# Four banks for a tile's sums, one run of new values, and a new order within a slot

## The chip, the cores and the metric

The kernel runs on one core of a Trainium2 chip. The metric is the device time of one execution in microseconds (us), the median of the runs shown. Times of single instructions are often given in nanoseconds (ns).

## The reference, cut to what matters

Four residual layers in a row over x of 64 batches x 32 rows x 512 features. The first and the last mix channels with a matrix chosen per batch, the second is a linear layer with a low-rank correction chosen per batch, and the third, where nearly all of the time goes, is attention with a paged cache:

```python
q = rope(rmsnorm(x @ Wq.T))        # 32 heads of 128; k and v have 8 heads
k, v = rope(rmsnorm(x @ Wk.T)), x @ Wv.T
k_all = concat(k_cache[block_table], k)   # 512 cached keys (16 pages of 32) + 32 new ones
v_all = concat(v_cache[block_table], v)
scores = where(valid, q @ k_all.T / sqrt(128), -1e30)
o = softmax(scores) @ v_all        # four query heads share one key head
x = x + o @ Wo.T
```

All data is fp32.

## The kernel before, in words

**Tiles, units, slots.** A tile is 128 rows of x, that is four batches. The key heads are done in two groups of four, so there are 2 x 16 = 32 steps of one group on one tile. A step has four units, one for each batch (`j` from 0 to 3), and a unit has four slots, one for each key head `k` of the group. A slot therefore handles one batch and one key head with its four query heads: 128 query rows (4 heads x 32 rows) against 544 keys. There are 32 x 4 x 4 = 512 slots, and the whole attention is one long list of them. In this text a slot is numbered by its place in that list; 16 slots make a tile, four make a unit.

**A slot's own pipeline.** `scores` (L832) makes 128 x 544 scores with two matmuls into a PSUM tile of two banks, `s_ps`, of which there is one; VectorE then adds the mask, and finds each row's extreme, in one pass (L846, called "the top" below: a pass of 128 x 544 with a short read of its accumulator), and ScalarE takes the exponential (L857). `divide` (L859) takes the reciprocal on VectorE (L862) and scales the cached part (L863) and the new part (L864) on ScalarE. Two slots later `flip` (L877) transposes the probabilities in four 128 x 128 pieces into the one bank `pT_ps` (tag "t" of the pool `ps_t`), and VectorE copies them to SBUF (L882). Three slots later `values` (L884) multiplies with the cached values in four accumulating matmuls (L893).

**What is done once in a unit.** `flip_new` (L866) transposes the new keys' probabilities of all four heads, in one 128 x 128 piece, into columns 0 to 127 of the *current* slot's score tile, which the scores leave unused; ScalarE copies them out (L875). It stands in the slot whose number is 1 modulo 4. `values_new` (L901) adds the new keys' values: four matmuls of 32 rows each (L905), one for each head, from four different row ranges into four different sums. `finish` (L913) copies the four sums to SBUF on ScalarE (L919, L922). After the fourth unit `store` (L927) writes the tile's 1 MB to DRAM with one DMA, on SP's queue except in the last three steps.

**PSUM.** Two banks hold the scores, one the flipped probabilities (tag "t"), one the projections (`proj_ps`), three the sums of the heads 0 to 2 (tag "o"), and the last one (tag "o3") is shared by the sum of head 3, the transposes of the query and key heads (`head_ps`, L750) and those of the second group's cache pages (`pageT_ps`, L266).

**What is interleaved.** Between these, the same slots carry the projections of the next pair of tiles. `Block.project` (L644) issues one matmul of 128 x 512 at a time (L651), one or two in nearly every slot. `Norm` (L697) turns the projected rows into normalized, rotated heads: squares on ScalarE (L707), a power on GpSimd (L712, L714), then the VectorE passes `scale`, `straight`, `swapped` and `sum` (L719 to L748, "pieces" below), the four transposes of `turn` (L756) and a copy on ScalarE, `keep` (L768).

**What sets the order.** The order is written out by hand, and every engine takes its instructions in the order in which the program issues them. `at(slot, where, ...)` puts a call into a plan and `slot(i)` (L1193) runs the plan for one slot, with these lines in the middle:

```python
            new.scores(k)
            turned.flip((i - LAG) % KG)
            run(i, "pe")                      # projections
            run(i, "take"); run(i, "late"); run(i, "power"); norm_piece(i)
            turned.flip_new()                 # every fourth slot
            run(i, "turn")                    # transposes of heads and pages
            old.values((i - VLAG) % KG)       # VLAG = 3, LAG = 2
            old.values_new()                  # every fourth slot, then at(i, "act", old.finish)
            new.divide(k)
            run(i, "dve"); norm_piece(i); norm_piece(i); run(i, "dve")
            run(i, "keep"); run(i, "act"); run(i, "store")
```

Two more places matter: GpSimd's queue gathers a unit's cached values, four gathers of 128 rows (`fetch_values`, L800, shown as L105), with eight buffers `v_sb` for two units; and SP's queue loads the cached keys page by page (L794) and a unit's new values (`fetch_new`, L813).

After the attention the output projection runs alone (L1301 to L1414).

## Time and profile before

| | |
|---|---|
| runs shown | 2476.70, 2469.84, 2477.28 us |
| their median | 2476.7 us |
| the profiled execution's own time | 2473.52 us |
| its span in the profile | 2471.8 us, so 1.7 us lie around it |
| TensorE clock granted | 0.999 |
| busy: TensorE matmul, weight load | 2438.3 us (99%), 1855.4 us (75%) |
| busy: VectorE, ScalarE, GpSimd | 1609.2 us (65%), 1398.3 us (57%), 1174.2 us (48%) |

The profile is of one execution. It has the busy time of each engine, a chain of waits that is followed back from the last instruction, groups of equal instructions with their mean durations, and a timeline. In it PE is TensorE's matmul, PEld TensorE's load of weights, DVE VectorE, ACT ScalarE, POOL GpSimd, SP SyncE; `s_ps L841` is what line 841 writes into the tile `s_ps`. An fp32 matmul shows as two matmuls, each with its own load of weights; a transpose shows as one. The durations of matmuls overlap, since they are pipelined: what one costs is read from the distance of the starts.

### The profile page before, as it was taken

The numbers are of one execution on the slowest core, as the hardware profiler recorded it, in microseconds if no ns is written. First come the engines' busy times: TensorE is split into PE (matmuls) and PEld (weight loads), VectorE is DVE, ScalarE is ACT, GpSimd is POOL, SyncE is SP. The second block draws the span as 40 slices with busy tenths as digits, with TensorE's granted clock in tenths as the row PEclk, the third lists the DMA queues.
The fourth block names the chain that finished last, engine by engine and source line by source line (L and its number), as shares of the span: only waits on it lengthen the run. The fifth ranks groups of instructions, "written<-read, shape, count | busy, mean of one in ns | idle before, by whom it ended". The sixth has DMA issues, their size and how long they took to land.

```text
span 2471.8 us, 47357 instructions
## 1 busy us (share of the span) xinstructions
PE 2438.3 (99%) x13760; PEld 1855.4 (75%) x13760; DVE 1609.2 (65%) x3602; ACT 1398.3 (57%) x4135; POOL 1174.2 (48%) x1096
## 2 busy tenths in 40 slices
PE   7999999999999999999999999999999999999999
PEld 4556777777777777777777777777777788888887
DVE  5767767676767677777777777777776756433222
ACT  2236767676767767677777777777676754000000
POOL 4436555455555565655556555555555753000000
PEclk9999999999999999999999999999999999999999
DMA  7876666666667677756666666565667784333221
GB/s 237 293 231 199 188 198 191 193 195 189 202 188 209 188 218 220 250 180 194 178 189 176 185 179 186 171 192 173 187 178 220 252 258 155 117 112 129 86 86 60
DMA packets 448545, 459.19 MB, mean 186 GB/s; under 512 B 51424, under 2 KB 379488, under 8 KB 440480
## 3 DMA queue, kind: packets, MB, share of 16 engines
q1 hardware_dynamic: 398384, 291.24, 38.1%
q0 software_dynamic: 49904, 164.93, 22.2%
q8 instruction: 112, 1.84, 0.3%
q14 instruction: 145, 1.19, 0.2%
HBM read 384.66 MB, written 79.69 MB: 188 GB/s over the span
## 4 chain that ended last, share of the span: by engine, by line
PE 95%; DMA 2%; issue 2%; SPq 1%; DVE 0%; POOL 0%; ACT 0%; DVEq 0%; POOLq 0%; ACTq 0%
PE proj_ps L651 23%; PE o_ps L893 18%; PE out_ps L1323 15%; PE s_ps L838 11%; PE s_ps L841 9%; PE pT_ps L880 9%; PE l_ps L490 3%; PE head_ps L756 3%; PE o_ps L905 2%; DMA kT<-kT 1%; PE h_ps L474 1%; SPq L794 1%; PE s_ps L873 1%; PE mix_ps L1341 1%; PE mix_ps L435 1%
## 5 line engine op out<-in xcount | busy, mean ns | idle before, releaser
L105 POOL DMA_INDIRECT v_sb<-v,v_rows x512 | 538.1, 1051 | 352.7 <-PE o_ps L893 242.8
L846 DVE CUSTOM_DVE_ANT_0 sm<-s_ps,pen 128x544 f32<-128x544 f32 x512 | 370.9, 724 | 457.9 <-PE s_ps L841 337.2
L893 PEld LDWEIGHTS o_ps<-pT,v_sb 128*128 128x128 f32 x4096 | 519.2, 192 | 133.6 <-issue 126.3
L857 ACT ACTIVATE sm<-sm,top 128x544 f32<-128x544 f32 x512 | 381.8, 746 | 339.6 <-DVE top L846 266.2
L893 PE MATMUL o_ps<-pT,v_sb 128*128 128x128 f32 x4096 | 541.4, 275 | 2.5 <-issue 1.3
L863 ACT ACTIVATE sm<-sm,share 128x512 f32<-128x512 f32 x512 | 369.8, 722 | 175.9 <-DVE share L862 144.2
L882 DVE COPY pT<-pT_ps 128x512 f32<-128x512 f32 x512 | 351.5, 687 | 8.0 <-PE pT_ps L880 4.1
L838 PE MATMUL s_ps<-kT,qT 128*128 128x288 f32 x1024 | 347.0, 420 | 2.8 <-DMA kT<-kT 2.1
L880 PE MATMUL pT_ps<-ident,sm 128*128 128x128 f32 x2048 | 307.7, 273 | 0.6 <-DVE pT L882 0.6
L841 PE MATMUL s_ps<-kT,qT 128*128 128x256 f32 x1024 | 305.3, 380 | 2.4 <-DMA kT<-kT 2.4
L880 PEld LDWEIGHTS pT_ps<-ident,sm 128*128 128x128 f32 x2048 | 256.1, 141 | 52.5 <-DVE pT L882 1.0
L809 POOL TENSOR_SCALAR pen<-key_f,seq_f 128x544 f32<-128x544 f32 x128 | 285.0, 2227 | 11.6 <-issue 0.3
L712 POOL TENSOR_SCALAR ss<-ss 128x4 f32<-128x4 f32 x160 | 56.4, 353 | 438.1 <-ACT sq L707 437.5
L841 PEld LDWEIGHTS s_ps<-kT,qT 128*128 128x128 f32 x1024 | 194.4, 190 | 57.2 <-issue 2.0
L663 DVE TENSOR_TENSOR raw<-proj_ps,raw 128x512 f32<-128x512 f32 x332 | 223.4, 685 | 18.7 <-PE proj_ps L651 13.9
L707 ACT ACTIVATE sq<-raw 128x128 f32<-128x128 f32 x640 | 197.2, 308 | 18.5 <-DVE raw L663 2.3
L714 POOL TENSOR_TENSOR rstd<-ss,minus_half 128x4 f32<-128x4 f32 x160 | 185.1, 1157 | 13.4
L1373 ACT COPY p<-out_ps 128x256 f32<-128x256 f32 x7 | 2.6, 373 | 333.1 <-PE out_ps L1323 333.1
L651 PE MATMUL proj_ps<-sum,x 128*128 128x512 f32 x380 | 186.9, 594 | 0.0
L105 POOL DMA_INDIRECT mix_rows<-in_w,cond_rows x32 | 33.0, 1031 | 309.3 <-DVE mix_diag L171 299.5
L838 PEld LDWEIGHTS s_ps<-kT,qT 128*128 128x128 f32 x1024 | 154.7, 191 | 20.0 <-issue 3.5
L1323 PE MATMUL out_ps<-w,o_in 128*128 128x256 f32 x768 | 167.1, 379 | 0.0
(175 smaller groups left out, 3492.7 us busy)
## 6 DMA issues: line engine op xcount, KB each, us to landing
kT<-kT SPq DMA_DIRECT2D x2048, 64.0 KB
o<-oT SPq DMA_DIRECT2D x29, 1024.0 KB
o_in<-o SPq DMA_DIRECT2D x28, 1024.0 KB
page_rows<-in_kv_cache SPq DMA_DIRECT2D x32, 256.0 KB
v<-in_kv_cache SPq DMA_DIRECT2D x32, 256.0 KB
kT<-page_rows SPq DMA_DIRECT2D x32, 256.0 KB
vn<-raw SPq DMA_DIRECT2D x32, 256.0 KB
v_sb<-v,v_rows POOLq DMA_INDIRECT x512
```

What stands on the lines that cost most here:

```text
L105: nc.gpsimd.indirect_dma_start(out=dst, out_offset=None, in_=table, in_offset=bass.IndirectOffsetOnAxis(ap=index, axis=0),)
L651: nc.tensor.matmul(self.ps, lhsT=self.pair.x[x][:, c if x == "b" else half.start + c, :], rhs=blocks(self.b)[w][:, c, :], start=(c == 0), ...
L809: nc.gpsimd.tensor_scalar(self.pen, key_f, seq_f[:, self.b : self.b + 1], BIG, ALU.is_ge, ALU.mult)
L838: nc.tensor.matmul(ps[:, first:HID], lhsT=q, rhs=self.kT[:, :n1, k, :], start=True, stop=True)
L841: nc.tensor.matmul(ps[:, HID : first + LA], lhsT=q, rhs=self.kT[:, n1:, k, :], start=True, stop=True)
L846: nc.vector.tensor_tensor_reduce(out=sm, in0=ps[:, first : first + LA], in1=self.pen, scale=1.0, scalar=3e38, op0=ALU.add, op1=ALU.min, ac ...
L857: nc.scalar.activation(sm, sm, AF.Exp, bias=top, scale=-1.0, accum_out=total)
L863: nc.scalar.activation(sm[:, :L], sm[:, :L], AF.Copy, scale=share)
L880: nc.tensor.transpose(ps[:, c, :], self.sm[k][:, c * P : (c + 1) * P], ident)
L882: nc.vector.tensor_copy(pT, ps)
L893: nc.tensor.matmul(self.o_ps[k], lhsT=self.v[c][:, k * D : (k + 1) * D], rhs=self.pT[k][:, c, :], start=(c == 0), stop=False,)
L1323: nc.tensor.matmul(ps[:, :HALF], lhsT=o[:, i, :], rhs=w[i // REP][:, i % REP, :], start=(i == 0), stop=(i == KG * REP - 1),)
```

## The change

- **Sums.** Each head of a tile has a bank of its own (tags o0 to o3) for all four units: `[128, 4, 128]`, one column range for each unit. Only the first matmul of a tile in a bank sets `start`.
- **New values in one go.** `values_new` is called for the four units one after the other, after the last `values` of the tile: 16 matmuls in a row, once in 16 slots, instead of four once in four slots. `v_new` and `pT_new` get four buffers each, and `fetch_new` is moved to the slots 4, 7, 10 and 13 of its tile.
- **finish and store.** They are called for each head of the tile: one copy of 128 x 512 each, two in the slot of the new values and two in the next one, to tiles `oT` of 256 KB with three buffers; four DMAs of 256 KB, those of the heads 0 and 1 on SP's queue and those of 2 and 3 on GpSimd's.
- **Order in a slot.** `values` (and `values_new`) come directly after the scores, then `flip_new`, `flip`, `divide`, and only then the projections and, last on TensorE, the transposes of heads and pages.
- **Bank.** Those transposes now use the bank of the flipped probabilities (tag "t"). The rule that kept them out of the slots of a unit's last head is gone.

```diff
--- before.py
+++ after.py
@@ -265,7 +265,7 @@
 
             def turn(self):
                 if self.g:
-                    self.ps = room["o"].tile([P, HID], F32, name="pageT_ps", tag="o3")
+                    self.ps = ps_t.tile([P, HID], F32, name="pageT_ps", tag="t")
                 else:
                     self.ps = ps_s.tile([P, 2 * HID], F32, name="s_ps")
                 for k in range(KG):
@@ -748,10 +748,7 @@
                 nc.vector.tensor_tensor(self.a, self.a, self.b, ALU.add)
 
             def turn(self):
-                if "o" in room:
-                    self.tp = room["o"].tile([P, REP, P], F32, name="head_ps", tag="o3")
-                else:
-                    self.tp = ps_t.tile([P, REP, P], F32, name="head_ps", tag="t")
+                self.tp = ps_t.tile([P, REP, P], F32, name="head_ps", tag="t")
                 for h in range(REP):
                     nc.tensor.transpose(self.tp[:, h, :], self.a[:, h, :], ident)
 
@@ -812,7 +809,7 @@
 
             def fetch_new(self):
 
-                self.v_new = room["v"].tile([P, D], F32, name="v_new", bufs=2)
+                self.v_new = room["v"].tile([P, D], F32, name="v_new", bufs=NB)
                 nc.sync.dma_start(
                     out=self.v_new,
                     in_=vn_dram[self.g][self.t][self.j * S : (self.j + 1) * S, :].rearrange(
@@ -827,7 +824,7 @@
                     step_of[self.s].kT_new[:, self.j].rearrange("p k s -> p (k s)"),
                 )
                 self.new = room["attn"].tile([P, KG, S], F32, name="p_new")
-                self.sm, self.total, self.pT, self.o_ps = {}, {}, {}, {}
+                self.sm, self.total, self.pT = {}, {}, {}
 
             def scores(self, k):
 
@@ -871,7 +868,7 @@
                 else:
                     ps = ps_s.tile([P, 2 * HID], F32, name="s_ps")[:, :P]
                 nc.tensor.transpose(ps, self.new.rearrange("p k s -> p (k s)"), ident)
-                self.pT_new = room["attn"].tile([P, P], F32, name="pT_new", bufs=1)
+                self.pT_new = room["attn"].tile([P, P], F32, name="pT_new", bufs=NB)
                 nc.scalar.copy(self.pT_new, ps)
 
             def flip(self, k):
@@ -884,18 +881,16 @@
             def values(self, k):
 
 
-                if k == 0:
-                    self.o_three = room["o"].tile([P, KG - 1, HID], F32, name="o_ps", tag="o")
-                    self.o_ps = {i: self.o_three[:, i, :P] for i in range(KG - 1)}
-                elif k == KG - 1:
-                    self.o_ps[k] = room["o"].tile([P, HID], F32, name="o_ps3", tag="o3")[:, :P]
+                if self.j == 0:
+                    o_of[self.s, k] = room["o"].tile([P, NB, P], F32, name="o_ps", tag=f"o{k}")
                 for c in range(NC):
                     nc.tensor.matmul(
-                        self.o_ps[k],
+                        o_of[self.s, k][:, self.j, :],
                         lhsT=self.v[c][:, k * D : (k + 1) * D],
                         rhs=self.pT[k][:, c, :],
-                        start=(c == 0),
+                        start=(self.j == 0 and c == 0),
                         stop=False,
+                        skip_group_check=True,
                     )
 
             def values_new(self):
@@ -903,30 +898,29 @@
                 for k in range(KG):
                     rows_k = slice(k * S, (k + 1) * S)
                     nc.tensor.matmul(
-                        self.o_ps[k],
+                        o_of[self.s, k][:, self.j, :],
                         lhsT=self.v_new[rows_k, :],
                         rhs=self.pT_new[rows_k, :],
                         start=False,
-                        stop=True,
-                    )
-
-            def finish(self):
-                if self.j == 0:
-                    oT_of[self.s] = room["attn"].tile([P, KG * REP, P], F32, name="oT", bufs=1)
-                dst = oT_of[self.s].rearrange("p (k h) s -> p k h s", k=KG)[
-                    :, :, :, self.j * S : (self.j + 1) * S
-                ]
-                nc.scalar.copy(
-                    dst[:, KG - 1], self.o_ps[KG - 1].rearrange("p (h s) -> p h s", h=REP)
-                )
-                nc.scalar.copy(
-                    dst[:, : KG - 1],
-                    self.o_three[:, :, :P].rearrange("p k (h s) -> p k h s", h=REP),
-                )
-
-            def store(self):
-                queue = nc.sync if self.s < len(steps) - 3 else nc.gpsimd
-                queue.dma_start(out=o_dram[self.g][self.t], in_=oT_of.pop(self.s))
+                        stop=(self.j == NB - 1),
+                        skip_group_check=True,
+                    )
+
+        def finish(s, k, copy):
+
+            o_ps = o_of.pop((s, k))
+            oT = oT_of[s, k] = room["attn"].tile([P, REP, P], F32, name="oT", bufs=3)
+            copy(
+                oT.rearrange("p h (j s) -> p h j s", j=NB),
+                o_ps.rearrange("p j (h s) -> p h j s", h=REP),
+            )
+
+        def store(s, k):
+            g, t = steps[s]
+            queue = nc.sync if k < 2 and s < len(steps) - 3 else nc.gpsimd
+            queue.dma_start(
+                out=o_dram[g][t][:, k * REP : (k + 1) * REP], in_=oT_of.pop((s, k))
+            )
 
 
 
@@ -942,7 +936,7 @@
                 do(*args)
 
         step_of, pair_of, unit_of, turn_of, first_of = {}, {}, {}, {}, {}
-        oT_of, rot_of = {}, {}
+        o_of, oT_of, rot_of = {}, {}, {}
         pieces = []
         busy = {}
         turning = set()
@@ -957,7 +951,7 @@
             piece()
             if norm:
                 slot += 1
-                while slot in turning or (slot - VLAG) % KG == KG - 1:
+                while slot in turning:
                     slot += 1
                 turning.add(slot)
                 at(slot, "turn", norm.turn)
@@ -1113,7 +1107,7 @@
             at(KG * (u - 1) + 1 if u else -1, "pool", call, unit_of, u, "mask")
             for c in range(NC):
                 at(KG * u - 1 + c, "pool", call, unit_of, u, "fetch_values")
-            at(KG * u - 1, "fetch", call, unit_of, u, "fetch_new")
+            at(u // NB * SLOTS + 4 + 3 * (u % NB), "fetch", call, unit_of, u, "fetch_new")
             at(KG * u - 2, "act", call, unit_of, u, "begin")
 
 
@@ -1197,27 +1191,31 @@
             if 0 <= i < n:
                 new = unit_of[i // KG]
                 new.scores(k)
+            if i >= VLAG:
+                old = unit_of[(i - VLAG) // KG]
+                old.values((i - VLAG) % KG)
+                if (i - VLAG) % SLOTS == SLOTS - 1:
+                    for u in range(old.u - NB + 1, old.u + 1):
+                        unit_of[u].values_new()
+                    for c in range(KG):
+                        last = old.s == len(steps) - 1
+                        copy = nc.vector.tensor_copy if last and c % 2 else nc.scalar.copy
+                        behind = i if last else i + c // 2
+                        at(behind, "act", finish, old.s, c, copy)
+                        at(behind + 1, "store", store, old.s, c)
             if LAG <= i < n + LAG:
                 turned = unit_of[(i - LAG) // KG]
+                if (i - LAG) % KG == KG - 1:
+                    turned.flip_new()
                 turned.flip((i - LAG) % KG)
+            if new:
+                new.divide(k)
             run(i, "pe")
             run(i, "take")
             run(i, "late")
             run(i, "power")
             norm_piece(i)
-            if LAG <= i < n + LAG and (i - LAG) % KG == KG - 1:
-                turned.flip_new()
             run(i, "turn")
-            if i >= VLAG:
-                old = unit_of[(i - VLAG) // KG]
-                old.values((i - VLAG) % KG)
-                if (i - VLAG) % KG == KG - 1:
-                    old.values_new()
-                    at(i, "act", old.finish)
-                    if old.j == NB - 1:
-                        at(i + 1, "store", old.store)
-            if new:
-                new.divide(k)
             if i >= 0:
                 run(i, "dve")
             norm_piece(i)
```

## Prediction

> **What bounds the kernel now.** I read the page first, its busy times and its chain of waits:
>
> ```profile
> PE 2438.3 (99%) x13760; PEld 1855.4 (75%) x13760; DVE 1609.2 (65%) x3602; ACT 1398.3 (57%) x4135; POOL 1174.2 (48%) x1096
> ...
> PE 95%; DMA 2%; issue 2%; SPq 1%; DVE 0%; POOL 0%; ACT 0%; DVEq 0%; POOLq 0%; ACTq 0%
> ```
>
> TensorE is the bound, and its stream has almost no holes. Other engines cost nothing as long as TensorE needn't wait for them. So the change is worth what it takes out of this stream, less what it makes the stream wait. The timeline of TensorE shows the price of each step as the distance of the starts (columns: start us, us, then the group):
>
> ```profile
> 1018.54 1.06 PE L893 MATMUL o_ps<-pT,v_sb 128*128 128x128 f32 x8
> 1019.44 0.65 PE L838 MATMUL s_ps<-kT,qT 128*128 128x288 f32 x2
> 1019.92 0.59 PE L841 MATMUL s_ps<-kT,qT 128*128 128x256 f32 x2
> 1020.36 0.60 PE L880 MATMUL pT_ps<-ident,sm 128*128 128x128 f32 x4
> 1020.79 1.06 PE L893 MATMUL o_ps<-pT,v_sb 128*128 128x128 f32 x8
> 1021.78 0.50 PE L905 MATMUL o_ps<-pT_new,v_new 32*128 32x128 f32 x8
> 1022.21 0.75 PE L838 MATMUL s_ps<-kT,qT 128*128 128x288 f32 x2
> 1022.80 0.59 PE L841 MATMUL s_ps<-kT,qT 128*128 128x256 f32 x2
> 1023.23 0.60 PE L880 MATMUL pT_ps<-ident,sm 128*128 128x128 f32 x4
> 1023.67 1.02 PE L651 MATMUL proj_ps<-wv,x_a 128*128 128x512 f32 x2
> ```
>
> Values take 0.89 to 0.90 us, scores 0.92 (0.48 + 0.44), flips 0.44, a projection matmul 0.86. But values followed by new values take 0.99, the new values 0.43, and the first score matmul after them 0.59 in place of 0.48: a unit's new values cost 0.09 + 0.43 + 0.11 = 0.63 us, of which the data stream is two passes of 0.11 (0.89 / 8), four row ranges abreast; 0.41 is the change into and out of 32-row matmuls.
>
> The third view is the timeline of all engines where TensorE comes to `flip_new` early, in a slot with little between:
>
> ```profile
> 1991.11 0.59 PE L841 MATMUL s_ps<-kT,qT 128*128 128x256 f32 x2
> 1991.54 0.60 PE L880 MATMUL pT_ps<-ident,sm 128*128 128x128 f32 x4
> ...
> 1991.74 0.72 DVE L846 CUSTOM_DVE_ANT_0 sm<-s_ps,pen 128x544 f32<-128x544 f32 x1 [1.20 <-PE s_ps L841]
> ...
> 1991.97 0.60 PE L1151 MATMUL proj_ps<-wo,o_in 128*128 128x256 f32 x2
> 1992.39 0.08 DVE L846 DVE_READ_ACCUMULATOR2_ANT top<- 128x1 f32 x1
> ...
> 1992.62 0.30 PE L873 MATMUL s_ps<-ident,p_new 128*128 128x128 f32 x1
> ...
> 1992.76 1.06 PE L893 MATMUL o_ps<-pT,v_sb 128*128 128x128 f32 x8
> ```
>
> The top starts 0.20 us after the scores' end (1991.54) and is done 0.93 after it (1992.39 + 0.08). `flip_new` waits for it: the values after it were due at 1991.97 + 0.43 + 0.11 = 1992.51 and start at 1992.76, 0.29 after the top's end. With one semaphore to wait for in place of two, the trace has the weight load 0.05 after the top's end rather than 0.11, so 0.22. In most slots this wait is hidden before: a projection's 0.86 us and the flips' 0.44 lie between.
>
> **What the Trainium skill says.** "TensorEngine Tiling (Array Packing)", Key Properties: changing the tiling mode drains TensorE. The trace agrees: the 0.41 us above. "TensorE: Matmul & The Clock Gate", Part 3, The mechanism: matmuls in different 32-row groups run concurrently; the eight of L905 in 0.43 us, against eight of L893 in 0.89, agree. "PSUM — Partial Sum Buffer", PSUM bank collisions raise a hardware error: guard PSUM by bank, not by address. So `flip_new` must wait for the top, though it writes columns that nothing reads; the trace shows the wait. The same page, Engine vs sequencer instructions: VectorE and ScalarE take their queues strictly in order; used in steps 3 and 5.
>
> **The change part by part.** After positions are from the built program's order. Signs: minus is saved.
>
> 1. *New values in one go.* Before: 128 units x 0.63 = 80.6 us. After: 32 blocks with one change (0.41) and eight passes of 0.11, so 1.29 us x 32 = 41.3. **-39 us.** The trace has no row of 16 in a row; bounds are 0 (drained again after each unit) and -39 (four abreast throughout; passes can't be shorter than their data). I take -39, since the second pass of a unit already follows the first without a hole.
>
> 2. *flip_new comes too early.* It now stands right behind the values, 0.89 us after the scores' end, and the flips are due at 1.00. The top ends at 0.93, so they start at 1.22 (79 units with two waits in the built program) or 1.15 (48). 79 x 0.22 + 48 x 0.15 = **+25 us**. Everything on TensorE is queued behind it. Nothing hides it: the projection that did has been moved behind.
>
> 3. *VectorE starts its tops late.* Its queue is strictly top, copy of the flips, reciprocal, pieces. Before, the flips end at 0.44 and the copy directly follows the top; now they end at 1.33, and VectorE idles from 0.85 to 1.53. Distances of starts in the trace: copy 0.60, reciprocal 0.07, a piece 0.60, `swapped` 0.7 to 0.8. So pieces begin at 2.21; in a slot with one projection and no heads (0.89 + 0.44 + 0.86 + 0.92) the next top is due at 3.11 + 0.20 = 3.31, and two pieces end at 3.41 (or 3.58 with `swapped`): it is 0.1 to 0.27 late. I went through the eight slots ahead of a `flip_new` in one window of 32: three such slots (0.09, 0.28, 0.27), one where four squares and two `finish` copies hold up the exponential, and so the reciprocal (0.6), four with two projections, heads or a single piece (0). Mean 0.16, on 127 units: **+20 us**. Bounds 0 and 45 (every slot late by 0.35).
>
> 4. *Heads in the flips' bank.* They now wait for the copy of the slot's own flips: 0.20 + 0.69 after the flips' end, and 0.11 until TensorE streams: 1.00. With one projection matmul between they are due at 0.86: 0.14 lost; with two (1.72), nothing. The built order has 125 head transposes and 16 page transposes behind a single one: 141 x 0.14 = **+20 us** (bounds 14 and 30, if the copy is late by step 3). The other way round, the next flips wait for ScalarE's `keep`; that is done about 0.6 us ahead of need, as scores and values (1.81 us) lie between.
>
> 5. *First values of a tile wait for finish.* Head 0's bank must be empty one slot after the new values. Slot of the new values: flips end at 0.89 + 1.27 + 0.44 = 2.60, the copy at 3.49, but the reciprocal starts behind it at 3.40; then on ScalarE scaling from 3.59 (0.63), new part (0.21), `begin` (0.19), and the first copy at 4.62, 0.56 long (as `qT L768`, of the same size): 5.18, and 0.11 until TensorE streams. The next slot's values are due at 2.60 + 0.86 + 0.92 = 4.38 with one projection (0.92 lost) or 5.24 with two (0.06). 16 tiles each: 14.7 + 1.0 = **+15 us**. Bounds 8 and 20.
>
> 6. *oT has three buffers for four heads.* ScalarE's copy for head 3 waits until the DMA of head 0 has landed; exponentials are queued behind it. No row has this 256 KB store; 1 MB stores land 5 to 9 us after issue in the trace, loads of 256 KB 2 to 4.5. The copy is free to start 3.7 us after head 0's, so it waits 0 to 1 us per tile; behind that are the exponential, the reciprocal, the pieces and a top. **+4 us**, bounds 0 and 18.
>
> 7. *values wait for the copy of the slot before.* 16 slots have no projection: due 0.92 after the flips' end, streaming at 1.00: **+1 us**. Elsewhere the 0.86 of a projection hides it.
>
> 8. *At nothing.* ScalarE: 256 copies (0.26 and 0.48) become 128 of 0.56, 22 us less on an engine that is 57% busy. SP has one store DMA more per tile (0.34 us), and v_new is fetched at least five slots ahead of use. GpSimd gets two store issues of 0.6 us per tile, which wait for ScalarE, with two gathers and a norm's power queued behind them. Those gathers are needed two to three slots (7 us and more) later, and TensorE waited for gathers 2.6 us in all before. If that cover were gone, a 2 us wait per tile would be 60 us. After the attention nothing changes.
>
> Sum: -39 + 25 + 20 + 20 + 15 + 4 + 1 = **+46 us**. The profiled execution took 2473.5 us (span 2471.8, 1.7 around it), so 2519.5. The runs' median is 3.2 us above it; that is within their spread, and I don't add it.
>
> **The rivals.**
>
> - *Faster: the waits are covered and the block alone counts.* TensorE's stream gets the 39 us of step 1 and VectorE, 65% busy, keeps up: 2473.5 - 39 = 2434. It decides if the added waits come to less than 39 / 512 = 0.08 us a slot. For it: the tops and copies are as short as before. Against it: a wait of just this kind cost 0.25 us at 1992.62. Chance 0.10.
> - *The gain and the waits nearly cancel.* Steps 2 and 4 hold, but VectorE catches up in the longer slots and `finish` is early (steps 3, 5 and 6 near their low ends): about +10, 2484. Chance 0.12, a bit over half of it within 0.3% of before, which is about what a measurement of this kernel can tell from no change.
> - *The sixteen don't stay abreast.* If TensorE changes over again after each unit, step 1 is 0, not -39: 2558. Chance 0.08; GpSimd's stores holding up gathers would look alike in the time.
>
> **How the numbers follow.** The forecast, 2491 to 2547, has 0.70: steps 3 to 6 at their bounds, not all at the same end, are some 28 us either way. To hold the time 8 times in 10 the range takes in the upper part of the cancelling case, from 2486. Faster 0.10, within 0.3% 0.07, slower 0.83.
>
> **What would show it.** In the profile of after: a block of new values 1.3 us long from its first start to the next step (step 1); PEld of `flip_new` idle on the top in nearly every unit (2), for 0.3 us or more where the top starts over 0.2 us after the scores (3); head transposes idle on DVE pT in slots with one projection (4); the first values of every second tile idle nearly 1 us on ACT oT (5); ScalarE's last copy of a tile waiting for the DMA of oT (6). I am wrong if these idle times together stay under 39 us, or if the block is near 2.5 us.

## The result and the profile after

The changed kernel takes 2575.7 us (median of 4 runs, 2570.9 to 2583.2) against 2475.5 us (median of the kernel before, now of 4 runs): 1.041 times the time before, 95% interval 1.038 to 1.044. The forecast was 2519.5 us with a range from 2486 to 2547. The direction was right and the size was not: +100 us came in place of +46. The profiled execution took 2575.5 us, span 2573.8.

The page of the changed kernel, the lines that answer to those of before, and the group of VectorE's copy, with that group of the kernel before below it:

```profile
PE 2465.0 (96%) x13760; PEld 1858.4 (72%) x13760; DVE 1635.7 (64%) x3604; ACT 1391.3 (54%) x4005; POOL 1169.1 (45%) x1163
...
PE 74%; DVE 9%; DMA 6%; ACT 5%; issue 4%; POOL 1%; SPq 0%; ACTq 0%; DVEq 0%; POOLq 0%
...
L879 DVE COPY pT<-pT_ps 128x512 f32<-128x512 f32 x512 | 353.8, 691 | 387.9 <-PE pT_ps L877 344.6
```

```profile
L882 DVE COPY pT<-pT_ps 128x512 f32<-128x512 f32 x512 | 351.5, 687 | 8.0 <-PE pT_ps L880 4.1
```

TensorE is no longer the whole chain: 74% where it was 95%, and VectorE, DMAs and ScalarE now each set the pace in places. VectorE stands 388 us ahead of its copy (8 us before), because the flips come late in a slot.

To see where the time went I took, for every matmul, the distance to the start of the one before it, less the distance that the same pair shows when nothing is late, and summed that by the step that starts late, minus the same for the kernel before. Before rounding these sums add up to 101.8 us; the spans differ by 102.0. All tables below are made so. A slot is counted within its tile, 0 to 15; "first values" are those of slot 3, which open a tile's sums, "other values" nearly all those of slots 7, 11 and 15, which open a unit.

| us more than before | new values | flip_new | flips | first values | other values | heads, pages | scores | projections | rest |
|---|---|---|---|---|---|---|---|---|---|
| changed kernel | -42 | +49 | +8 | +29 | +28 | +25 | -2 | +2 | +6 |

The block of new values, on TensorE's timeline:

```profile
886.76 1.05 PE L887 MATMUL o_ps<-pT,v_sb 128*128 128x128 f32 x8
887.74 1.17 PE L900 MATMUL o_ps<-pT_new,v_new 32*128 32x128 f32 x32
888.85 0.66 PE L877 MATMUL pT_ps<-ident,sm 128*128 128x128 f32 x4
889.34 1.02 PE L651 MATMUL proj_ps<-sum,x_b 128*128 128x512 f32 x2
```

The 32 passes take 888.85 - 887.74 = 1.11 us, four abreast throughout. Around them lie 0.09 us ahead (values at 0.98 in place of 0.89) and 0.05 behind (flips 0.49 in place of 0.44): 1.25 us, forecast 1.29.

And the timeline of all engines in the slot in which `flip_new` waits longest on average, slot 5 of the second tile of a pair:

```profile
896.25 0.58 ACT L913 COPY oT<-o_ps 128x512 f32<-128x512 f32 x1 [0.43 <-DMA o<-oT]
...
898.03 0.31 ACT L707 ACTIVATE sq<-raw 128x128 f32<-128x128 f32 x1
...
898.34 0.73 ACT L854 ACTIVATE sm<-sm,top 128x544 f32<-128x544 f32 x1
898.52 0.23 POOL L712 TENSOR_SCALAR ss<-ss 128x4 f32<-128x4 f32 x1 [6.00 <-ACT sq L707]
...
899.20 0.16 DVE L859 RECIPROCAL share<-total 128x1 f32<-128x1 f32 x1 [1.78 <-ACT sm L854]
...
899.86 1.24 POOL L921 DMA_DIRECT2D o<-oT  x2
899.87 0.68 DVE L719 TENSOR_TENSOR raw<-raw,rstd 128x512 f32<-128x512 f32 x1
...
900.47 0.72 DVE L843 CUSTOM_DVE_ANT_0 sm<-s_ps,pen 128x544 f32<-128x544 f32 x1
...
901.25 0.33 PE L870 MATMUL s_ps<-ident,p_new 128*128 128x128 f32 x1 [1.03 <-DVE top L843]
901.41 1.05 POOL L105 DMA_INDIRECT v_sb<-v,v_rows  x1 [0.30 <-issue]
```

Read it backwards. `flip_new` stands 1.03 us for the top; the top is late because VectorE's two pieces stand behind the reciprocal; the reciprocal waited 1.78 us for the exponential; and that stood behind four squares on ScalarE, which stood behind the last copy of the sums (896.25), which had waited 0.43 us for the DMA of `oT`. On GpSimd the gather begins at 901.41, behind two stores (899.86), which stand behind the norm's power, which waited 6.00 us for the same squares. The waits of TensorE and of GpSimd, in total (columns: us, times, longest):

```profile
PE s_ps L870 <- DVE top L843: 28.5, 47, 1.6
PE o_ps L887 <- ACT oT L913: 21.1, 29, 1.1
PE o_ps L887 <- DMA v_sb<-v,v_rows: 16.5, 16, 4.9
```

```profile
POOL ss L712 <- ACT sq L707: 518.7, 153, 9.2
...
POOL o L921 <- ACT oT L913: 132.4, 20, 22.0
```

In the kernel before:

```profile
PE o_ps L893 <- DMA v_sb<-v,v_rows: 1.2, 1, 1.2
```

```profile
POOL ss L712 <- ACT sq L707: 437.5, 155, 6.7
```

GpSimd waited 20.9 us for `oT` there. (Part of a wait shows on TensorE's weight load instead; the table above has both.)

### The profile page after: what moved, and what is told of

Its sections match the earlier page's. It is cut to its first block, busy times and chain, and to the rows that moved or that the text cites. A ratio compares the mean times of both kernels' runs of the same rounds, so it can differ in the third digit from the quotient of the medians.

```text
span 2573.8 us, 47058 instructions
## 1 busy us (share of the span) xinstructions
PE 2465.0 (96%) x13760; PEld 1858.4 (72%) x13760; DVE 1635.7 (64%) x3604; ACT 1391.3 (54%) x4005; POOL 1169.1 (45%) x1163
## 3 DMA queue, kind: packets, MB, share of 16 engines
q14 instruction: 145, 1.19, 0.2%
## 4 chain that ended last, share of the span: by engine, by line
PE 74%; DVE 9%; DMA 6%; ACT 5%; issue 4%; POOL 1%; SPq 0%; ACTq 0%; DVEq 0%; POOLq 0%
PE proj_ps L651 16%; PE out_ps L1321 14%; PE o_ps L887 13%; PE pT_ps L877 8%; PE s_ps L835 6%; PE s_ps L838 6%; DMA v_sb<-v,v_rows 3%; PE head_ps L753 3%; PE l_ps L490 3%; DMA o<-oT 2%; ACT sq L707 2%; DVE pT L879 2%; DVE sm L843 2%; DVE rot_a L748 1%; PE s_ps L870 1%
## 5 line engine op out<-in xcount | busy, mean ns | idle before, releaser
L887 PEld LDWEIGHTS o_ps<-pT,v_sb 128*128 128x128 f32 x4096 | 536.2, 191 | 89.2 <-ACT oT L913 33.3
L887 PE MATMUL o_ps<-pT,v_sb 128*128 128x128 f32 x4096 | 553.5, 277 | 42.1 <-ACT oT L913 21.1
L835 PE MATMUL s_ps<-kT,qT 128*128 128x288 f32 x1024 | 334.5, 408 | 2.9 <-DMA kT<-kT 1.5
L835 PEld LDWEIGHTS s_ps<-kT,qT 128*128 128x128 f32 x1024 | 180.1, 191 | 149.4 <-issue 142.8
L806 POOL TENSOR_SCALAR pen<-key_f,seq_f 128x544 f32<-128x544 f32 x128 | 275.8, 2155 | 11.4
L712 POOL TENSOR_SCALAR ss<-ss 128x4 f32<-128x4 f32 x160 | 39.8, 249 | 519.3 <-ACT sq L707 518.7
L877 PEld LDWEIGHTS pT_ps<-ident,sm 128*128 128x128 f32 x2048 | 239.7, 141 | 5.5 <-POOL pen L806 1.7
L838 PEld LDWEIGHTS s_ps<-kT,qT 128*128 128x128 f32 x1024 | 194.7, 190 | 53.9
L714 POOL TENSOR_TENSOR rstd<-ss,minus_half 128x4 f32<-128x4 f32 x160 | 167.7, 1048 | 13.3
```

The costliest lines, as they stand in the source:

```text
L806: nc.gpsimd.tensor_scalar(self.pen, key_f, seq_f[:, self.b : self.b + 1], BIG, ALU.is_ge, ALU.mult)
L835: nc.tensor.matmul(ps[:, first:HID], lhsT=q, rhs=self.kT[:, :n1, k, :], start=True, stop=True)
L838: nc.tensor.matmul(ps[:, HID : first + LA], lhsT=q, rhs=self.kT[:, n1:, k, :], start=True, stop=True)
L877: nc.tensor.transpose(ps[:, c, :], self.sm[k][:, c * P : (c + 1) * P], ident)
L887: nc.tensor.matmul(o_of[self.s, k][:, self.j, :], lhsT=self.v[c][:, k * D : (k + 1) * D], rhs=self.pT[k][:, c, :], start=(self.j == 0 and ...
```

## The experiments

All times are medians beside runs of the kernel before on the same chip (2473.5 to 2474.3 us). The table gives what each cost on TensorE over the kernel before, by step; e1 to e8 change one thing of the changed kernel or go back to the old order, e9 to e16 build on one another.

| | time | ratio (95%) | new values | flip_new | flips | first values | other values | heads | scores | projections |
|---|---|---|---|---|---|---|---|---|---|---|
| e1 | 2613.5 | 1.055-1.059 | -42 | -3 | +3 | +29 | +16 | +17 | +113 | +1 |
| e2 | 2521.5 | 1.017-1.021 | -39 | -1 | +2 | -1 | +6 | +51 | -1 | +27 |
| e3 | 2508.1 | 1.010-1.016 | -39 | -1 | +33 | -1 | +9 | 0 | -1 | +29 |
| e4 | 2590.7 | 1.045-1.050 | -42 | +50 | +10 | +49 | +16 | +26 | -1 | +5 |
| e5 | 2562.0 | 1.033-1.040 | -42 | +12 | +3 | +30 | +58 | +18 | 0 | +5 |
| e6 | 2544.7 | 1.026-1.031 | -42 | +45 | +8 | -1 | +29 | +25 | -2 | +2 |
| e7 | 2598.8 | 1.048-1.052 | -42 | +63 | +9 | +46 | +11 | +27 | +3 | +3 |
| e8 | 2609.0 | 1.053-1.058 | -42 | +39 | +54 | +28 | +21 | +27 | -4 | 0 |
| e9 | 2516.4 | 1.016-1.019 | -42 | +4 | +3 | 0 | +51 | +16 | +1 | +3 |
| e10 | 2546.4 | 1.027-1.032 | -42 | +4 | +53 | -1 | +44 | -1 | +4 | +4 |
| e11 | 2520.2 | 1.017-1.020 | -42 | +3 | +69 | -2 | +7 | 0 | +5 | +2 |
| e12 | 2533.9 | 1.023-1.027 | -42 | +3 | +69 | 0 | +13 | -1 | +4 | +3 |
| e13 | 2468.8 | 0.997-0.999 | -42 | +5 | +4 | -2 | +7 | +17 | +3 | +1 |
| e14 | 2474.9 | 0.999-1.001 | -42 | +4 | +19 | -2 | +10 | -1 | +7 | +1 |
| e15 | 2494.0 | 1.005-1.009 | -13 | +3 | +15 | -2 | +7 | -1 | +4 | 0 |
| e16 | 2468.1 | 0.996-0.998 | -42 | +3 | +9 | -2 | +9 | -1 | +6 | +5 |

My first theory was that the slot's order carries the loss, through the wait of `flip_new` for the top, and that the banks and the one go alone would gain. Its rival: with the banks as changed, any order pays.

**e1, flip_new late.**

```diff
-                if (i - LAG) % KG == KG - 1:
-                    turned.flip_new()
                 turned.flip((i - LAG) % KG)
...
             norm_piece(i)
+            if LAG <= i < n + LAG and (i - LAG) % KG == KG - 1:
+                turned.flip_new()
             run(i, "turn")
```

> The changed kernel with one thing undone: flip_new goes back behind the projections, ahead of the heads. Theory (a wait on the top, exposed by the place of flip_new, costs some 50 us): 2525 us, and TensorE's idle time of flip_new on the top falls from 54 us to under 5. Rival (VectorE is late anyway, and whatever comes next on TensorE waits in its place): 2560 or more, with the idle time now at the scores or the heads.

38 us slower than the changed kernel, not 50 faster. The wait on the top is gone, and a dearer one came:

```profile
PE s_ps L835 <- ACT pT_new L872: 62.2, 88, 1.6
```

`flip_new` writes into the score bank, so the next scores wait until ScalarE has copied it out. In the kernel before, the values stood between; now they come first in a slot, and behind a late `flip_new` there is nothing but the scores, with heads between in some slots. The rival had the place, the next scores, but not the cause: it is ScalarE's copy, not a late VectorE. So in this order `flip_new` can come too late as well as too early.

**e2, the old order with the new banks** (new values still in one go):

```diff
+            if LAG <= i < n + LAG:
+                turned = unit_of[(i - LAG) // KG]
+                turned.flip((i - LAG) % KG)
+            run(i, "pe")
...
+            if LAG <= i < n + LAG and (i - LAG) % KG == KG - 1:
+                turned.flip_new()
+            run(i, "turn")
             if i >= VLAG:
...
-            if LAG <= i < n + LAG:
...
-            run(i, "turn")
```

> The banks and the new values in one go as changed, but the slot in the order of before: scores, flips, projections, flip_new, heads, values, new values. Theory (the order carries the loss, the one go alone is a gain): -39 for the block, +20 for heads that still wait for the copy of the flips, a few us for gathers, so 2455 to 2465 us. Rival (sharing the flips' bank, the finish copies of four heads and the stores on GpSimd carry the loss whatever the order): 2490 or more.

2521.5 us: the theory fell, since a loss of 48 us stays in the old order; the new order adds 54 to it. The one go brings 39 us, and what comes with it (the shared bank, the copies and stores by head) costs more. The heads lose 51 us in the flips' bank (the flips then end 0.44 us behind the scores, so by an estimate from the distances in the prediction their copy stands behind the top and is done at 0.93 + 0.69 = 1.62, while the heads come at 0.44 + 0.86 = 1.30). And projections lose 27:

```profile
PE proj_ps L651 <- ACT raw L671: 17.8, 15, 2.0
PE head_ps L753 <- DVE pT L879: 14.1, 49, 1.4
```

The projection bank is emptied by a ScalarE copy (L671) that is queued behind the new `finish` copies. ScalarE stands at the first of these for TensorE's end signal 27.2 us in 12 waits.

**e3, heads behind the values,** on top of e2:

```diff
-            run(i, "turn")
             if i >= VLAG:
...
             if new:
                 new.divide(k)
+            run(i, "turn")
```

> As the old order, but the heads go behind the values: scores, flips, projections, flip_new, values, new values, heads. Theory (heads lose only because too little lies between the copy's flips and them): the 20 us of the heads goes too, 2440 us. Rival (the next slot's flips then wait for ScalarE's copy of the heads, as scores alone lie between): 2460 or more, with idle time of the flips on ACT.

The heads wait no more, but the next flips wait for ScalarE's keep (+33): the rival's answer. The shared bank is used by two pairs of writer and reader, and whichever stands close behind the other waits.

**e4, all stores on SP.**

```diff
-            queue = nc.sync if k < 2 and s < len(steps) - 3 else nc.gpsimd
+            queue = nc.sync if s < len(steps) - 3 else nc.gpsimd
```

> The changed kernel with all four stores of a tile issued by SP in place of two by GpSimd. Theory (GpSimd stands at its stores until ScalarE's last copies, and the gathers behind it land late: the waits on v_sb in slots 7 and 15 of a tile, 28 us): 2548 us, waits on v_sb under 8 us. Rival (the values come 1.3 us earlier in a slot and outrun the gathers whoever stores): 2570 or more.

15 us slower than the changed kernel: the rival's side in time. The waits for gathers fell by 12 us of 28, so GpSimd's stores are some of them, and 16 stay, as the rival says. But what made it slower is neither: the first values lost 20 more, with VectorE's copy behind the block 2.3 us late in 12 tiles (last section).

**e5, flip_new one step later.**

```diff
-                if (i - LAG) % KG == KG - 1:
-                    turned.flip_new()
                 turned.flip((i - LAG) % KG)
+                if (i - LAG) % KG == KG - 1:
+                    turned.flip_new()
```

> The changed kernel with flip_new one step later: behind the flips, ahead of the projections. Theory (flip_new costs only because it comes before the top is done; 0.44 us of flips cover that, and a projection behind it covers ScalarE's copy): the 51 us of flip_new on the top and the 5 at the flips go, 2522 us. Rival (as when it stood behind the projections, the next scores wait for ScalarE's copy out of their bank): 2550 or more, with idle time of the scores on ACT pT_new.

`flip_new` and the flips lost 42 us less, as the theory says, and heads 7 less. But the kernel gained only 14, and the waits tell where the rest went:

```profile
PE o_ps L887 <- DMA v_sb<-v,v_rows: 40.4, 32, 4.2
...
PE s_ps L870 <- DVE top L843: 9.5, 13, 1.2
```

TensorE came earlier to the values that open a unit, and there stood for the gathers: 58 us in place of 28. The wait for the top had covered them. This is neither of my two theories; the gathers were the next bound.

**e6, the first head's copy early.**

```diff
-                        at(behind, "act", finish, old.s, c, copy)
+                        if c == 0:
+                            finish(old.s, c, copy)
+                        else:
+                            at(behind, "act", finish, old.s, c, copy)
```

> The changed kernel with ScalarE's copy of the first head's sums put straight behind the exponential, ahead of the slot's scaling, so it no longer waits for the copy of the flips and the reciprocal. Theory (the 30 us at the first values of a tile come from this queue): idle time of values in slot 3 of a tile falls from 30 to under 8 us, 2550 us. Rival (TensorE's own end signal is late where a gather runs, so that ScalarE starts no sooner in every second tile): 15 us or more stay, 2562.

31 us faster, and the first values' 29 us are gone to the last. The theory holds: these waits come from ScalarE's queue, in which the copy stood behind the scaling, hence behind the reciprocal and VectorE's copy. The late end signal that the rival names is there (in 12 tiles the early copy starts more than 2.5 us after the block's start, elsewhere at 1.2 to 1.4), but TensorE no longer waits for it. And as the first DMA of `oT` now starts earlier, ScalarE's wait for it falls from 5.1 us to 0.2, with 4 us less at `flip_new` (step 6 below).

**e7, gathers early.**

```diff
-                at(KG * u - 1 + c, "pool", call, unit_of, u, "fetch_values")
+                at(KG * u - 1 + (c + 1) // 2, "pool", call, unit_of, u, "fetch_values")
```

> The changed kernel with the four gathers of a unit issued over two slots after the first in place of three (none of them in the slot of the new values' block). Theory (values outrun the gathers, and a gather that runs beside the block makes TensorE's end signal late): the 26 us of waits for v_sb fall under 8, the late signals in every second tile go as well (13 us), 2540 us. Rival (GpSimd stands at its stores, and the gathers are late whatever their place): 2568 or more.

The other values' wait fell from 28 to 11 us, so the place of the gathers does decide it. But `flip_new` lost 14 us more and the first values 17 more, and the time rose by 23. In this run VectorE's copy behind the block was late by 2.3 us in 12 tiles (last section).

**e8, heads at the start of the next slot.**

```diff
-                slot += 1
+                slot += 2
...
             run(i, "pool")
+            if i >= 0:
+                run(i, "turn")
+                run(i, "keep")
             new, k = None, i % KG
```

> The changed kernel with the heads' transposes and ScalarE's keep at the start of the next slot, ahead of the scores, in place of behind the projections. Theory (heads wait only for VectorE's copy out of the shared bank, which by then is done): their 23 us go, 2552 us. Rival (the shared bank moves the wait: the flips wait for ScalarE's keep, or the heads for VectorE's sum): 2568 or more.

A badly made experiment: the start of a slot is the same place on TensorE as the end of the slot before, so the heads kept their 27 us. What it did move is ScalarE's keep, behind the four squares, and the flips then waited 54 us for it. That taught where the keep must not stand.

**e9, both e5 and e6.**

> The changed kernel with both: flip_new behind the flips, and the first head's copy ahead of the scaling. Theory (two separate costs, but what is saved at flip_new goes in part to the gathers): -14 and -31 as each alone, 2530 us, with waits for v_sb near 55 us. Rival (the gathers bound the slots now, and take what the early copy saves as well): 2545 or more.

2516.4 us, 59 us less than the changed kernel where the two alone give 45, with 51 us left at the gathers. The gathers don't take what the first copy saves, so the rival fell.

**e10, heads between scores and values,** on top of e9:

```diff
                 new.scores(k)
+                run(i, "turn")
+                run(i, "keep")
+                new.top(k)
...
-                slot += 1
+                slot += 2
```

`new.top` is the second half of `scores`, from VectorE's pass on, so that ScalarE's keep comes ahead of the exponential.

> As the last, and the heads between scores and values two slots behind their sum, ScalarE's keep ahead of the exponential. Theory (between them and the flips lie 0.86 + 0.92 us on one side and 0.89 on the other, so neither the heads nor the flips wait for the shared bank): the 18 to 23 us of the heads go, 2510 us. Rival (the time is given back at the gathers, which set the pace): 2525 or more, with v_sb waits over 60 us.

The heads' wait is gone (16 to -1), the flips' wait for the keep is 53 us. The rival named the wrong resource, but it is slower, as it said.

**e11, the fourth gather one slot earlier,** on top of e10, and **e12, all stores on SP,** on top of e10:

```diff
-                at(KG * u - 1 + c, "pool", call, unit_of, u, "fetch_values")
+                at(KG * u - 1 + min(c, 2), "pool", call, unit_of, u, "fetch_values")
```

> As the last, and a unit's fourth gather issued one slot earlier, behind the third. Theory (the values come too early for the fourth gather of a unit, which is what the forecast held to be covered): v_sb waits under 15 us, 2470 us. Rival (two gathers back to back on GpSimd delay TensorE's end signals and the norms' powers, so VectorE is later): v_sb waits fall but flip_new and the first values wait more, 2500 or more.

> As the heads between scores and values, gathers as in the changed kernel, with all stores of a tile on SP. Theory (GpSimd's stores hold up the gathers): v_sb waits under half of those without it, 2490 us. Rival (SP gets to its stores late, oT comes free late, and ScalarE's copies wait for it): the same time or slower, with idle time at oT.

The fourth gather alone takes the other values from 44 to 7 us, the stores from 44 to 13, as the two theories say of the waits. But in both the flips then wait 69 us for the keep, 16 more than in e10, and the times are 2520 and 2534 in place of 2470 and 2490: a rival that neither expectation had.

**e13, e9 with the fourth gather one slot earlier** (heads as in the changed kernel).

> The changed kernel with flip_new behind the flips, the first head's copy ahead of the scaling, and a unit's fourth gather one slot earlier; heads as in the changed kernel. Theory (the waits for v_sb, 55 us without the third edit, come from the fourth gather alone): v_sb under 10 us, 2476 us. Rival (gathers back to back delay VectorE and the norms, and flip_new or the first values take it): 2495 or more.

2468.8 us, 0.998 times the kernel before (0.997 to 0.999). Three small edits to the order, none to the banks, undo the whole loss of 100 us, as the theory says. The third alone, from e9 to e13, is worth 48 us. The wait for `v_sb`, in e9 and then in e13:

```profile
PE o_ps L887 <- DMA v_sb<-v,v_rows: 43.0, 35, 4.3
```

```profile
PE o_ps L887 <- DMA v_sb<-v,v_rows: 4.0, 7, 1.1
```

Page of e13:

```profile
PE 2423.1 (98%) x13760; PEld 1854.2 (75%) x13760; DVE 1639.1 (66%) x3604; ACT 1393.3 (56%) x4005; POOL 1173.4 (47%) x1163
...
PE 88%; DVE 4%; ACT 3%; DMA 3%; issue 1%; SPq 1%; POOL 0%; DVEq 0%; ACTq 0%; POOLq 0%
```

**e14, heads clear of the squares,** e11 with

```diff
-                while slot in turning:
+                while slot in turning or slot % 32 in (6, 8, 12, 17, 18, 20, 23, 27, 29, 30, 31):
```

> The same three edits, and the heads between scores and values, but never in a slot in which ScalarE runs the four squares. Theory (the 70 us that flips waited for ScalarE's keep are slots where the keep stood behind the squares, 1.7 us): flips under 15 us, heads 0, 2465 us, faster than the kernel before. Rival (the keep ahead of the exponential makes the exponential, the reciprocal and so the tops late everywhere): 2490 or more.

The flips' wait fell from 69 to 19 us, so the squares ahead of the keep were the cause; the time, 2474.9, is that of the kernel before, between the two.

**e15, new values by unit,** on top of e14:

```diff
-                if (i - VLAG) % SLOTS == SLOTS - 1:
-                    for u in range(old.u - NB + 1, old.u + 1):
-                        unit_of[u].values_new()
+                if (i - VLAG) % KG == KG - 1:
+                    old.values_new()
```

> As the last, with each unit's new values behind its own values again, in the same four banks. Theory (step 1: three more changes into and out of 32-row matmuls per tile): 96 x 0.41 = 39 us slower than the last. Rival (part of these changes lie in time that TensorE waits anyway): less than 25 us slower.

```profile
813.46 1.05 PE L891 MATMUL o_ps<-pT,v_sb 128*128 128x128 f32 x8
814.45 0.50 PE L904 MATMUL o_ps<-pT_new,v_new 32*128 32x128 f32 x8
814.88 0.66 PE L881 MATMUL pT_ps<-ident,sm 128*128 128x128 f32 x4
815.37 1.02 PE L651 MATMUL proj_ps<-wk,x 128*128 128x512 f32 x2
```

A unit's new values cost 0.10 + 0.43 + 0.05 = 0.58 us here, so by the timeline the one go saves 32 x (4 x 0.58 - 1.25) = 34 us (29 of them show in the table at the new values, 5 at the flips behind them). The whole kernel is only 19 us slower: the longer slots of e15 cover waits that e14 has, so the flips' waits, the other values and the scores cost less. The rival's number, with the mechanism it named.

**e16, heads clear of one copy more** (e14 with 11 added to the list).

> As the kernel with the heads clear of the squares, and the heads also kept out of the slot in which ScalarE's copy of the first product runs at its start. Theory (the 10 us that flips still waited in slot 11 of a tile are this copy ahead of the keep): 2464 us, flips' waits near 10 us. Rival (the heads crowd into other slots and wait there): 2474 or more.

2468.1 us, 0.997 times the kernel before (0.996 to 0.998). The flips' wait halved, as expected; 4 us of it went to the projections of that slot. e13 and e16 are faster than both kernels, by a quarter of a per cent.

## Why the prediction fell short

Step by step, as it was put there:

- **Step 1, new values in one go, -39: right.** -42 in the block, +3 at the flips behind it.
- **Steps 2 and 3, flip_new too early and tops late, 25 + 20 = 45: right,** 49 + 5 = 54 us measured (the flips' +8 less the 3 of step 1), some 6 of which belong to step 6, so 48. Two slots of every second tile stand out: slot 5, behind squares, with 0.7 us before the wait of step 6 is added, and slot 9, with 0.5 to 1.0 us in nearly all; I had one such slot, at 0.6 + 0.22. What I had not priced is the way out: e1 shows that a later place meets the score bank.
- **Step 4, heads in the flips' bank, +20: right,** 25 us including the pages.
- **Step 5, first values wait for finish, +15: the mechanism was right and half the size missing.** 29 us. In the tiles with one projection the stall is 0.87 us in most (0.78 to 1.30), forecast 0.92, and 0.1 more at the next weight load. In those with two I forecast 0.06; 12 of 14 show 0.85 to 0.92, the two others nothing. In exactly these 12 VectorE's copy behind the block starts 0.9 us late, though it stood idle, since TensorE's end signal was late. (One tile at the end, with shorter matmuls in place of the projections, shows 0.87 too.) With the copy ahead of the scaling (e6) the stall is gone in all of them.
- **Step 6, three buffers, +4: right, some 6 us.** ScalarE waited 5.1 us for the DMA of `oT`, in 12 waits, and 11 of these reach TensorE along the path that the step names, at the `flip_new` of slot 5 (timeline above). In the four whole tiles without such a wait it costs 0.7 us there, in the 11 with one 0.9 to 1.7. In e6, where the waits are gone, it is about 0.7 in all of them. **Step 7, +1:** TensorE waited 2.3 us for `pT` at values.
- **Step 8, at nothing: this step failed,** in its sentence that the gathers are needed two to three slots later. That is true of a unit's second and third gathers (the first has four slots). The fourth is planned in the slot just ahead of the unit's first values, and these the change brought forward by the flips' 0.44 and a projection's 0.86 us; GpSimd's stores pushed the gathers back besides. 28 us in place of 0, and 58 once `flip_new` no longer hid part of it (e5). e13 shows it alone: one gather moved by one slot is worth 51 - 7 = 44 us there. The prediction did name the price if that cover were gone (60 us), but put it in no range or chance of its own; it only noted that it would look in time like the rival to which it gave 0.08. I had counted the slack of the earlier gathers and not of the last.
- **Step 8 also said that nothing changes after the attention:** TensorE waits 4.8 us there for the last copies of the sums (0.8 before).

The two large parts of the miss, steps 5 and 8, are 14 + 28 = 42 us. Steps 2 to 4 came out 3 + 5 above their sums, step 6 some 2, and the time after the attention 4: 56 us, what is missing. Some 10 of step 5's 14 go with a late end signal whose cause stays open (last section).

The rivals: the sixteen did stay abreast. Its time (2558) was nearest to the result, but by luck: what it describes did not happen, and only part of the miss has the reason that the prediction mentions beside it, GpSimd's stores holding up gathers. Single cures don't add up here: e5 alone gave 14 us of its 42, e7, which moves gathers alone, made things worse, and e13, which has e5, e6 and one gather moved, gave 107 (2575.7 - 2468.8).

## What to carry to other kernels

When a step is moved forward in a pipelined slot, count the slack of the last transfer that it needs, not of the first, and count it on the queue that issues it. A stall that is removed hands its time to the next late arrival, so price a change with that arrival named; here a cure worth 42 us at its place was worth 14 while the gathers stood next in line. A bank shared by two writers needs both turnarounds (write, copy, next write) laid out in the slot, and a long group in the copying engine's queue, such as four squares, must not stand ahead of either copy.

## What the runs showed of the hardware

**TensorE's end signals can come late, for a reason that stays open.** In the changed kernel, TensorE's and VectorE's lines of one block of new values, and the same tile in e9:

```profile
826.54 1.17 PE L900 MATMUL o_ps<-pT_new,v_new 32*128 32x128 f32 x32
827.65 0.65 PE L877 MATMUL pT_ps<-ident,sm 128*128 128x128 f32 x4
828.14 1.88 PE L651 MATMUL proj_ps<-sum,x 128*128 128x512 f32 x4
```

```profile
829.18 0.69 DVE L879 COPY pT<-pT_ps 128x512 f32<-128x512 f32 x1 [2.58 <-PE pT_ps L877]
```

```profile
805.99 1.88 PE L651 MATMUL proj_ps<-sum,x 128*128 128x512 f32 x4
```

```profile
806.19 0.69 DVE L879 COPY pT<-pT_ps 128x512 f32<-128x512 f32 x1 [1.75 <-PE pT_ps L877]
```

The copy starts 806.19 - 805.99 = 0.20 us after the flips' end in e9, the usual distance, and 829.18 - 828.14 = 1.04 us after it in the changed kernel, while VectorE stands idle. The trace's semaphore events agree: TensorE's increments that were due 1.0 to 1.8 us after the block's start are all recorded from 2.4 us on. In the changed kernel this is so in 12 blocks, and in exactly those GpSimd begins the second of two gathers back to back 0.93 us after the block's start. In e4 and e7, with three gathers in a row there, the copy was 2.3 us late. But e9 has the same two gathers at the same distance and no delay in any block, so the gathers alone don't make it. The delay is there in 12 blocks with e5's edit alone and in 12 with e6's alone; with both, in e9 to e16, VectorE's copy is late in none. That may be some of the 14 us by which e9 beats the sum of the two; no run separates it. In the changed kernel the delay goes with stalls of some 10 us (12 x 0.87, an estimate from step 5). In e2, in the old order, ScalarE's wait at its first copy of the sums is of the same kind: in 13 tiles it starts over 2.5 us after the block's start, in the others mostly after 1.19.

**Matmuls of 32 rows from four row ranges keep four abreast for 32 passes:** 1.11 us, where eight passes of a single unit take 0.43. If each pass costs the same, that is (1.11 - 0.43) / 24 = 0.028 us a pass, so that of the 0.43 some 0.23 are the eight passes, and the other 0.2 are paid once a run at both lengths. This is an estimate from two lengths; no third was run.
